# The second tail scores of a batch, issued ahead of the last slot block of the third pair of heads

## The chip, the cores and the metric

The kernel runs on one core of a Trainium2 chip. The metric is the device time of one execution in microseconds; the median of the runs counts. The engines are named as in the profile: PE (matrix multiplier) with PEld (its weight loads), DVE (vector engine), ACT (scalar engine, which does the exponentials), POOL (issues the row gathers and scatters), SP (issues the other transfers, in order). A line number such as L756 is a line of the kernel.

## The reference

Sixteen batches of 512 channels by 1024 tokens pass through one attention layer with 8 heads of 64, with keys and queries masked per token, and the layer's result is added to the input. Query, key and value are the same projection.

```python
xt = jnp.transpose(x, (0, 2, 1))
q = xt @ Wq.T
qh = q.reshape(B, T, NH, dk).transpose(0, 2, 1, 3)
scores = scale * jnp.einsum('bhqd,bhkd->bhqk', qh, qh)
logits = (scores * cmask + (1.0 - cmask) * NEG) * rmask
attn = jax.nn.softmax(logits, axis=-1)
ctx = jnp.einsum('bhqk,bhkd->bhqd', attn, qh)
out = ctx.transpose(0, 2, 1, 3).reshape(B, T, D) @ Wo.T
x = x + jnp.transpose(out, (0, 2, 1))
```

A masked query gets all logits zero, so its result is the mean of all values. A live query attends to the live keys alone. About half of the tokens are live.

## The kernel before, in words

**What is computed.** For each batch the kernel gathers the live tokens' rows into *slots* and works on these. A batch has `wide[b]` slots: 544 in batches 0 to 4, 528 in 5 to 13, 512 in 14 and 15. The first 512 are four *slot blocks* of 128; what is beyond, 32 or 16 slots, is the *tail*. Fourteen batches have one. The rows of masked tokens get the mean, added by `rest` (L874).

**Scores.** `scores(b, p, i)` (L653) with a block `i` of 0 to 3 takes one head `p`: four matmuls (L693) into a PSUM buffer `pss`, then one exponential on ACT (L697) into a tile `p`, with the row sums into `z`. There are two `pss` buffers, used in turn, and twelve `p` tiles. With `i` None it does a whole tail for four heads at once: 16 matmuls of 32 columns (L668), one exponential (L672), with row sums into `zt`; DVE then splits the result into a high part `hi` (L677) and a low part `lo` (L678), and four transfers (L684, L685) spread both over a tile `pt`, of which there is one. The first tail scores of a batch serve heads 0 to 3, the second heads 4 to 7.

**Attention and normalisation.** `attend(b, p, i, ps)` (L702) multiplies a block's probabilities with the values, for a pair `p` of heads (two of the eight heads; pairs 0 to 3): 8 matmuls L718 a block, 32 a pair. With `i` 4 it adds the tail from `pt` (L722) and copies the sum to a tile `c` (L726). Each pair needs reciprocals of its row sums: `recip_sums` (L734) computes them on DVE into `rcol` (L741 takes `z`, L747 takes `zt`, then L748, L749, L750); `recip_rows` (L752) transposes `rcol` on PE (L756), copies it out (L759, `rr`), writes it to DRAM (L761, `rd`) and reads it back spread over the partitions (L765, `rb`). `norm` (L769) multiplies `c` by `rb` (L791) and splits the result to 16 bits. `product` (L801) is the output projection: 12 matmuls L809 a slot block, whose result `plus` (L813, L814) adds to the gathered rows.

**The order.** `run` (L925) writes the order out by hand. A batch is a list `S` of 18 steps: the 16 blocks, pair by pair, and two tails put in between. In a step it runs first what the step before left for later (the transfers of `pt` and of the next queries' `xx`) and what the table `free` holds for this step's number; then the scores of the even head, a part of the list `m`, the scores of the odd head, one row transfer for POOL, another part of `m`. In a tail's step it is the tail scores and one part of `m`. The list `m` holds the rest of the work: of the batch before, the last normalisations and the projection; of the next batch, the row transposes (L481, with `xsplit`, L439 and L440), the query projections (L508), the values (L565), the row maxima (`top`, L620, and `bottom`, L629). How much of `m` goes into a part is set by costs that are written beside its entries and by the table `share` (L1100): 1.2 for a tail, 0.9 and 0.9 for the last block of a pair, 0.9 and 1.0 for the third, 1.0 and 0.6 for the first.

The attend matmuls of a pair run in the next pair's second block (L1131 to L1136), those on its tail in that pair's third block. `recip_sums` and `recip_rows` of the pairs 0 to 2 hang on the number `st` of the step of the pair's last block, `norm` of pair 2 runs in the next batch (from `second`, L1043), in batch 15 in the last step:

```python
                    if i == 3:
                        (whole if p < 3 else todo).append(L(self.attend, b, p, 4, None))
                        if p < 3:
                            free.setdefault(st + 2, []).append(L(self.recip_sums, b, p))
                            free.setdefault(st + 3, []).append(L(self.recip_rows, b, p))
```

**The planner.** The program is written in this order, and a framework then makes each engine's stream from it, before the run: at each point an engine takes, of what is ready by the framework's own estimate, what was written first. So DVE operations of neighbouring steps are found interleaved in the trace. On the chip an engine's stream is fixed.

Of the kernel before, what the change touches and what calls it, by code (L numbers as in the profile page):

```python
# [46 lines left out]
class Fast:  # L47
# [877 lines left out]
    def run(self, flag):  # L925
        B = self.B
        L = lambda f, *a: lambda: f(*a)
        S = [(p, i) for p in range(NP) for i in range(4)]
        S.insert(2, (0, None))
        S.insert(13, (1, None))  # L930
        N = len(S)

        def xt(n):
# [361 lines left out]
```

## Time and profile before

| | us |
|---|---|
| runs: median of three | 1044.05 |
| runs: lowest, highest | 1043.74, 5687.53 |
| profiled execution | 1045.58 |
| its span, first to last instruction | 1043.8 |

The granted clock of the profiled execution was 0.995. A batch takes about 62 us; the first tail scores of batch 5 start at 356.26 us and the second at 393.50, those of batch 6 at 419.73 and 458.56. The profile gives each engine's busy time, groups of instructions by line with their mean duration and the idle time ahead of them, and what ended that idle time. A wait for several things is put down to the one that came last by the profile, and it names the wrong one at times; the ends of matmuls are modelled, their starts are measured.

### The profile page before, as it was taken

To read this page: it belongs to the slowest core of one execution; us is meant where nothing else is said; L and a number is where in the kernel's file an instruction comes from. 1 tells how busy PE (TensorE), PEld (TensorE's weight loads), DVE (VectorE), ACT (ScalarE), POOL (GpSimd) and SP (SyncE) were. 2 spreads that over 40 slices of the span, in tenths; PEclk is the share of its full clock that TensorE was granted. 3 is DMA by queue.
4 is the path that set the end of the run, shared out by engine and by line. 5 is a ranking of instruction groups with operands and counts; after the bars stand their busy time and mean duration, and the time that the engine had idled before them with its cause. 6 is when DMAs were issued, how large, how long until landed. Compare 5 with 4: busy or idle time off the path is not lost. (4 is left out here: it accounts for less than half of the span.)

```text
span 1043.8 us, 23675 instructions
## 1 busy us (share of the span) xinstructions
PE 994.7 (95%) x8527; PEld 692.3 (66%) x8527; DVE 720.9 (69%) x2408; ACT 656.4 (63%) x1702; POOL 299.5 (29%) x308
## 2 busy tenths in 40 slices
PE   7798999999999999999999999999999999999995
PEld 6576667666666766667676666766767676776552
DVE  7897668666766657767666777667678675756562
ACT  5876666666666665757666557665766666655650
POOL 3101023223301222233222223223333322325652
PEclk9899999999999999999999999999999999999999
DMA  6756555557645576666558656565665566546641
GB/s 212 215 142 175 138 152 166 164 156 207 189 125 149 135 214 176 166 189 163 164 159 233 183 141 188 152 192 175 202 193 153 164 172 183 154 132 195 201 170 74
DMA packets 78796, 177.74 MB, mean 170 GB/s; under 512 B 14688, under 2 KB 20576, under 8 KB 78672
## 3 DMA queue, kind: packets, MB, share of 16 engines
q1 hardware_dynamic: 57584, 108.40, 38.3%
q0 software_dynamic: 21088, 67.75, 20.7%
q8 instruction: 70, 1.15, 0.5%
q14 instruction: 54, 0.44, 0.1%
HBM read 91.49 MB, written 33.91 MB: 120 GB/s over the span
## 5 line engine op out<-in xcount | busy, mean ns | idle before, releaser
L697 ACT ACTIVATE p<-pss,nm 128x528 f32<-128x528 f32 (+2 forms) x512 | 359.9, 707 | 190.6 <-PE pss L693 181.1
L693 PE MATMUL pss<-xx 128*128 128x264 f16 (+2 forms) x2048 | 302.7, 277 | 8.2 <-ACT p L697 7.0
L718 PE MATMUL pav<-p,v 128*64 128x264 f32 (+2 forms) x2048 | 243.3, 390 | 0.0
L693 PEld LDWEIGHTS <-xx 128*128 128x128 f16 x2048 | 195.0, 99 | 63.9 <-issue 26.8
L718 PEld LDWEIGHTS pav<-p,v 128*64 128x64 f32 x2048 | 141.4, 137 | 85.7 <-issue 13.3
L893 POOL DMA_INDIRECT y_out<-xa,idx x68 | 73.7, 1083 | 284.7 <-PE pss L693 129.4
L508 PE MATMUL pm<-xh,wqh 128*128 128x264 f16 (+5 forms) x512 | 142.4, 278 | 4.1 <-DVE xa L814 2.3
L508 PE MATMUL pm<-xl,wqh 128*128 128x264 f16 (+5 forms) x512 | 141.7, 277 | 0.2 <-DVE xl L440 0.2
L508 PE MATMUL pm<-xh,wql 128*128 128x264 f16 (+5 forms) x512 | 141.9, 277 | 0.0
L390 POOL DMA_INDIRECT xa<-x_in,idx x68 | 67.9, 998 | 203.1 <-PE pss L693 89.6
L508 PEld LDWEIGHTS <-wqh 128*128 128x128 f16 x1024 | 98.1, 99 | 24.5 <-issue 7.5
L697 ACT ACTIVATION_READ_ACCUMULATOR p<-pss,nm 128x1 f32 x512 | 104.1, 203 | 0.0
L893 POOL DMA_INDIRECT y_out<-xi,idx x60 | 71.5, 1192 | 101.4 <-PE pss L693 38.1
L809 PE MATMUL pm<-woh,ch 128*128 128x512 f16 x240 | 91.1, 379 | 0.0
L809 PE MATMUL pm<-woh,cl 128*128 128x512 f16 x240 | 90.9, 379 | 0.0
L809 PE MATMUL pm<-wol,ch 128*128 128x512 f16 x240 | 90.9, 379 | 0.0
L390 POOL DMA_INDIRECT xi<-x_in,idx x60 | 61.7, 1029 | 97.3 <-PE pss L693 33.8
L511 ACT ACTIVATE q<-pm 128x264 f32<-128x264 f32 (+5 forms) x128 | 50.3, 393 | 60.1 <-PE pm L508 59.8
L809 PEld LDWEIGHTS <-ch 128*128 128x128 f16 x480 | 45.9, 98 | 44.7 <-issue 0.9
L814 DVE SCALAR_TENSOR_TENSOR xa<-pm,xa 128x512 f32<-128x512 f32 x60 | 41.3, 688 | 44.3 <-PE pm L809 40.6
L880 DVE TENSOR_TENSOR xi<-xi,ub 128x512 f32<-128x512 f32 (+1 forms) x60 | 40.7, 687 | 44.2 <-PE pss L693 41.7
L791 DVE TENSOR_TENSOR c<-c,rb 128x528 f32<-128x528 f32 (+2 forms) x64 | 45.4, 710 | 32.8 <-PE pm L508 16.3
(220 smaller groups left out, 1511.4 us busy)
## 6 DMA issues: line engine op xcount, KB each, us to landing
xx<-hl SPq DMA_DIRECT2D x224, 136.0 KB
xm<-x_nat_in SPq DMA_DIRECT2D x56, 512.0 KB
rb<-rd SPq DMA_DIRECT2D x72, 132.0 KB
rb<-rd SPq DMA_DIRECT2D x40, 136.0 KB
pt<-c SPq DMA_DIRECT2D x36, 132.0 KB
pt<-p SPq DMA_DIRECT2D x36, 132.0 KB
ub<-ud SPq DMA_DIRECT2D x16, 256.0 KB
xx<-hl SPq DMA_DIRECT2D x32, 128.0 KB
```

What stands on the lines that cost most here:

```text
L390: dma = self.nc.gpsimd.indirect_dma_start(out=tile[:n], out_offset=None, in_=self.x, in_offset=bass.IndirectOffsetOnAxis(ap=idx, axis=0))
L508: self.beat = nc.tensor.matmul(pq, lhsT=w[:, c, e * P:(e + 1) * P], rhs=xx[:, c, cols], start=(k == 0), stop=(k == 3 * DC - 1)).ins
L511: nc.scalar.activation(s["q"][:, e, cols], pq, AF.Copy, scale=1.0 / (SX * SW))
L693: self.beat = nc.tensor.matmul(pt[:, g, :CH], lhsT=xx[:, 2 * k, i * P:(i + 1) * P], rhs=xx[:, 2 * k + a, g * CH:(g + 1) * CH], start=(a == ...
L697: self.exp = [nc.scalar.activation(t.rearrange("p (g c) -> p g c", g=2), pt[:, :, :CH], AF.Exp, bias=s["nm"][p // HG][:, p % HG:p % HG + 1 ...
L718: mm = nc.tensor.matmul(s["pav"][k * DK:(k + 1) * DK, g, :CH], lhsT=s["v"][p][:, i, k * DK:(k + 1) * DK], rhs=ps[k][:, cols], start=(i == ...
L791: self.once(nc.vector.tensor_tensor(c[:, :A], c[:, :A], s["rb"][p], ALU.mult), self.beat if p < 3 else None)
L809: nc.tensor.matmul(po[:cols.stop - cols.start], lhsT=a[:, e, cols], rhs=w[:, e, :], start=(e == 0 and k == 0), stop=(e == DC - 1 and k == 2))
L814: self.nc.vector.scalar_tensor_tensor(x, po, 1.0 / (SX * SW), x, ALU.mult, ALU.add)
L880: self.once(self.nc.vector.tensor_tensor(x[:n], x[:n], s["ub"][:n], ALU.add), self.beat)
L893: dma = self.nc.gpsimd.indirect_dma_start(out=self.out, out_offset=bass.IndirectOffsetOnAxis(ap=idx, axis=0), in_=x, in_offset=None)
```

## The change

The second tail is put into the list of steps one place earlier.

```diff
         S = [(p, i) for p in range(NP) for i in range(4)]
         S.insert(2, (0, None))
-        S.insert(13, (1, None))
+        S.insert(12, (1, None))
         N = len(S)
```

| step | before | after |
|---|---|---|
| 10, 11 | pair 2, blocks 1 and 2 | the same |
| 12 | pair 2, block 3 | second tail |
| 13 | second tail | pair 2, block 3 |
| 14 to 17 | pair 3, blocks 0 to 3 | the same |
| `recip_sums` of pair 2 | step 14 | step 15 |
| `recip_rows` of pair 2 | step 15 | step 16 |

The last two lines follow from `st + 2` and `st + 3`, as the block's own step is now 13. The entries of `free` that have a fixed number (loads of the batch after next at steps 0, 3, 6 and 9, their row sums on ACT at 4, 7, 10 and 13; in batch 0 the loads at 4, 7, 10 and 13) keep it: what is at step 13 now comes behind the tail and ahead of the block. In the two batches without a tail, the tail's step issues its part of `m` alone, and the `recip` steps of pair 2 move as in the others.

## The prediction

> **What bounds the kernel now.** I read the page first, then the windows by stage, the waits, and the timeline around the tail.
>
> ```profile
> PE 994.7 (95%) x8527; PEld 692.3 (66%) x8527; DVE 720.9 (69%) x2408; ACT 656.4 (63%) x1702; POOL 299.5 (29%) x308
> ...
> L697 ACT ACTIVATE p<-pss,nm 128x528 f32<-128x528 f32 (+2 forms) x512 | 359.9, 707 | 190.6 <-PE pss L693 181.1
> L693 PE MATMUL pss<-xx 128*128 128x264 f16 (+2 forms) x2048 | 302.7, 277 | 8.2 <-ACT p L697 7.0
> ```
>
> ACT waits 181.1 us for the scores; PE waits 7.0 us for ACT. The windows (length; then busy time with instruction count of PE, PEld, DVE, ACT, POOL; clock; DMA) say where PE is not full:
>
> ```profile
> 0.00:36.00 36.00, 28.02 (x298) 23.48 (x299) 26.70 (x100) 23.68 (x61) 12.47 (x33) 1.00 0.74 234
> 417.00:917.00 500.00, 487.33 (x4251) 342.58 (x4250) 352.76 (x1222) 322.65 (x838) 148.41 (x142) 1.00 0.62 174
> 979.00:1044.00 65.00, 51.10 (x342) 28.85 (x340) 27.61 (x71) 21.91 (x58) 30.00 (x28) 0.96 0.43 145
> ```
>
> In the eight batches of the middle line (about 62 us each) PE idles 12.67 us, 1.6 us a batch. Nothing but those gaps can be won by a new order, and nothing is lost unless PE gets new ones. Where are they near the tail? In batch 4 (start, duration, engine, line and what it does, idle before it):
>
> ```profile
> 333.81 0.30 DVE L747 TENSOR_TENSOR rcol<-zt,corr 32x1 f32<-32x1 f32 x2
> ...
> 334.87 0.28 PE L629 MATMUL pm<-ident,m 128*128 128x4 f32 x2
> ...
> 335.58 0.17 DVE L750 TENSOR_TENSOR rcol<-rcol,hit 128x10 f32<-128x10 f32 x1
> ...
> 335.89 0.30 PE L756 MATMUL pm<-ident,rcol 128*128 128x128 f32 x1 [0.74 <-ACT p L697]
> ```
>
> PE has passed L629 at 334.90 and stands until 335.89, with 0.10 us usual after an L629. The view names ACT, but L750, which writes what L756 reads, ends at 335.75, 0.14 us ahead. That is the wait. L756 is `recip_rows` of pair 2, and its sums take L747's operand `zt` from the exponentials of the second tail: tail scores 331.85, their exp 332.57 to 333.4, L747 333.81, L750, L756. The same 0.14 to 0.15 us stands between L750's end and L756 in batches 1, 3, 4, 6, 7, 9, 10, 12 and 13. One more wait on this tail, in batch 0, and one beside it:
>
> ```profile
> 87.75 0.49 PE L722 MATMUL pav<-pt,vt 128*128 128x272 f32 x2 [2.18 <-DMA pt<-p]
> ...
> 398.39 0.27 PE L508 MATMUL pm<-xh,wqh 128*128 128x264 f16 x1 [0.56 <-DVE xa L814]
> ```
>
> **The change, part by part.** Nothing is added or removed: 16 tail matmuls, one exp, two DVE operations and four `pt` transfers swap places with one slot block (8 matmuls, two exps). Fourteen batches have the tail. But the index of the block goes from 12 to 13, and `recip_sums` and `recip_rows` of pair 2 hang on that index: steps 14 and 15 become 15 and 16.
>
> *(A) The wait at L756.* The tail's exp comes a block (some 3 us) earlier, L756 one step later, behind the 32 attend matmuls of step 15 (336.59 to 340.08 in batch 4). With 3.5 to 4.4 us more between them and a need of 0.9, the wait goes. From the starts of L629 and L756: 0.96, 0.96, 0.99, 1.02, 1.01, 1.01, 1.01, 1.02 us in eight batches, less 0.10 each, 7.2 us; batch 13 adds 0.9: −8.1 us.
>
> *(B) Batch 0's `pt`.* The transfers were issued at 81.26 to 83.97 and PE stood 2.18 us for them. The tail moves up by the block that ran 71.98 to 74.93, some 3 us: −2.2. If the SP queue keeps them behind the `xx` transfers of 76.48 to 79.4, the gain is between 0 and −2.2; I take −2.0.
>
> *(C) L508 behind L814.* 2.3 us in all by the waits on L814, because DVE ran the tail's two operations (0.43 and 0.71) just before L814. They move ahead, but `project`, whose result L814 takes, may land between tail and block and meet them again: 0 to −2.3; I take −1.0, half.
>
> *(D) What is issued earlier or later with it.* The PSUM buffers of the scores alternate: the tail now waits for the exp of the block before, the moved block for the tail's, each an exp of 0.9 us on ACT. The trace has 15 waits of this kind among 512 half blocks, 7.0 us, 0.47 each. One fewer in a few batches would be −1, one more in each of 14 batches +6.6; I take four more, +2. On SP the four `pt` issues pass nothing but the `xx` transfers of the next query (396.22 to 398.62 in batch 5), whose reader runs some 10 us later. On POOL the row transfers keep one issue a step, and hang on the tail's last matmul in place of the block's: no PE work waits for them. ACT's row sum (L420, 1.24 us) changes from ahead of the tail's exp to ahead of the block's: cover is the 190.6 us in which ACT waits anyway.
>
> *(E) The later reciprocal.* L756 starts the chain copy, `rd` to DRAM, `rb` back, `norm` of pair 2 (L791) early in the next batch. In batch 5:
>
> ```profile
> 399.38 0.64 SPq L685 DMA_DIRECT2D pt<-p  x1
> 400.07 0.78 SPq L684 DMA_DIRECT2D pt<-c  x1
> 400.90 0.80 SPq L685 DMA_DIRECT2D pt<-p  x1
> 401.80 0.48 SPq L761 DMA_DIRECT2D rd<-rr  x1
> 407.03 1.10 SPq L765 DMA_DIRECT2D rb<-rd  x2
> ...
> 412.15 0.71 DVE L791 TENSOR_TENSOR c<-c,rb 128x528 f32<-128x528 f32 x1
> ```
>
> Here `rd` takes 5.23 us because it follows 528 KB of `pt`; for pair 1, with nothing ahead, 1.28 (388.42 to 389.70). Now L756 runs at 399.74 and L791 at 412.15, 12.4 us on. Moved behind the attends it would run at about 404.55, 7.6 us ahead of L791. The shortest chain in the trace, the last batch's, is 6.5 us (L756 1022.59, L791 1029.12, DVE idle 5.94 us for it). With the `pt` transfers already gone, 6.5 fits into 7.6: cost 0, and the cover left is 1.1 us. At the very end L791 of pair 2 (1014.34) would come about 3 us later, near 1017.5, its results near 1020.3, and PE takes them with the matmuls from 1021.28: 0 to +1 us, taken as 0.
>
> Sum: −8.1 −2.0 −1.0 +2 = −9.1 us.
>
> Should PE gaps count in full? The row: PE busy 97.5% in the middle window, and an L693 starts every 0.113 us without a pause. [...] The trace sides with the row, since the other engines wait for PE.
>
> The profiled execution took 1045.58 us (span 1043.8 and 1.8 around it), 1.5 over the median of 1044.05; the same sum taken off the median is 1044.05 − 9.1 = **1035 us**.
>
> **The rivals.**
> *1. The reciprocal comes too late (slower).* If `rd` still takes 5.23 us (behind `xx` or `xm` transfers), the chain is 6.5 + 4.0 = 10.5 against 7.6, and `norm` is 2.9 us late; if the whole shift of 4.8 us arrives, 4.8. Behind L791 on DVE stand L440 (413.52 to 414.80), which free the buffers for the transposes PE wants at 417.08: 2.3 us of cover. So from 2.3 us on it decides; at 4.8 PE loses 2.5 us in each of 13 batches, +32 us, less the 9: 1044 + 23 = 1067. For: 1.1 us of margin is small. Against: the `pt` bytes ahead of `rd` are what made it slow, and the planner places L791 by its own estimate of readiness. DVE ran nothing in the 5.94 us before the last L791. [...]
> *2. The gaps move (no change).* PE reaches the next buffer that DVE or ACT must free 0.9 us sooner and waits there. For: in batch 5's timeline DVE has no pause over 0.39 us from 390.75 to 402.4. Against: after L756 follow 3.5 us of attends, for which DVE need do nothing. A's 8.1 is paid again: 1035 + 8.1 = 1043; up to 1050 where D is at its end.
> *3. More is won.* All of A, B, C and none of D is −12.6, 1031; half of what is left of the 1.6 us a batch once A is out (8.1 over 14 is 0.6, so 1.0) is −7 more: 1024.
>
> **How the numbers follow.** Forecast (1031 to 1041) 0.52; gaps move (1041 to 1050) 0.28; late reciprocal (1050 to 1071) 0.13; more won 0.07. The range of 8 in 10 is 1029 to 1054: forecast, second rival and the nearer part of the first, 0.84. About 2%, 21 us, is what a measurement of this kernel can tell from no change: below 1023 only beyond rival 3, 0.04; above 1065 the far half of rival 1, 0.09; else 0.87.
>
> **What would show it.** A: L756 of pair 2 behind 32 L718, with no idle before it in batches 1, 3, 4, 6, 7, 9, 10, 12, 13. B: L722 near 86 us without its 2.18. C: the L814 entry of L508 below 2.3. E: second `rb` issue to L791 still near 4 to 5 us, `rd` to `rb` near 1.3 to 2.7 for pair 2, no DVE idle over 0.5 us before L791. It is wrong if PE's middle-window busy time does not rise, or if idle before L440 or L481 appears early in each batch.

## The result, and the profile after

| | before | after |
|---|---|---|
| median, us (16 runs each) | 1043.07 | 1050.47 |
| lowest, us | 1040.44 | 1045.18 |
| span of the profiled execution, us | 1043.8 | 1049.1 |

The changed kernel takes 1.0063 times the time of the one before (95% interval 1.0047 to 1.008): 0.6% slower, where 0.9% faster was forecast. This ratio is not the quotient of the medians (1.0071): it is worked out from the fast runs alone, which leaves out one run of 5687.53 us of the kernel before. Its interval, 0.33% wide, tells 0.6% from no change, where the prediction had allowed for 2%. First the page of after (busy us, share of the span; then groups with busy time, mean ns of one, and idle time ahead with what ended it):

```profile
PE 1000.3 (95%) x8527; PEld 693.9 (66%) x8527; DVE 719.4 (69%) x2408; ACT 653.7 (62%) x1702; POOL 298.6 (28%) x308
...
L693 PE MATMUL pss<-xx 128*128 128x264 f16 (+2 forms) x2048 | 303.8, 277 | 12.0 <-ACT p L697 6.4
...
L508 PE MATMUL pm<-xh,wqh 128*128 128x264 f16 (+5 forms) x512 | 142.7, 279 | 6.6 <-DVE xa L814 5.9
...
L791 DVE TENSOR_TENSOR c<-c,rb 128x528 f32<-128x528 f32 (+2 forms) x64 | 45.3, 708 | 56.6 <-DMA rb<-rd 21.7
```

Of before, a group and a line of the view of waits (us in all, times, longest):

```profile
L508 PE MATMUL pm<-xh,wqh 128*128 128x264 f16 (+5 forms) x512 | 142.4, 278 | 4.1 <-DVE xa L814 2.3
DVE c L791 <- DMA rb<-rd: 8.9, 7, 2.6
```

and from the windows of after:

```profile
417.00:917.00 500.00, 488.08 (x4241) 341.41 (x4239) 352.61 (x1226) 320.94 (x838) 149.63 (x142) 1.00 0.61 174
```

In the middle window PE is busy 488.08 us of 500, against 487.33: nearly as many gaps as before. PE's wait for L814 has gone from 2.3 to 5.9 us, all the idle time ahead of L693 from 8.2 to 12.0. L791's waits for `rb` are 21.7 us, 8.9 before.

**The wait at L756 is gone.** PE in batch 4 (start, duration, engine, line and what it does):

```profile
341.01 0.28 PE L629 MATMUL pm<-ident,m 128*128 128x4 f32 x2
...
347.25 0.28 PE L508 MATMUL pm<-xh,wql 128*128 128x266 f16 x1
347.36 0.27 PE L756 MATMUL pm<-ident,rcol 128*128 128x128 f32 x1
347.47 0.63 PE L693 MATMUL pss<-xx 128*128 128x272 f16 x4
```

L756 runs 6.3 us behind the L629 it followed directly before, 0.11 us from its neighbours on both sides, with no idle in brackets. The chain behind it, in batch 5 (SP and DVE in the timeline of after):

```profile
402.13 0.74 SPq L685 DMA_DIRECT2D pt<-p  x1
...
410.87 0.32 SPq L761 DMA_DIRECT2D rd<-rr  x1
412.16 1.62 SPq L765 DMA_DIRECT2D rb<-rd  x2
...
417.72 0.71 DVE L791 TENSOR_TENSOR c<-c,rb 128x528 f32<-128x528 f32 x1
```

`rd` takes 1.29 us to its `rb`, as forecast, in place of 5.23: the `pt` transfers are long gone.

**Batch 0 loses 5.9 us in the profiled execution.** The first attend matmul (L718) of batch 0 starts at 50.1 us before and 49.2 after, that of batch 1 at 115.2 and 120.2: this stretch takes 65.1 and 71.0. It begins on SP. The timeline of before, then of after:

```profile
76.48 0.48 SPq L536 DMA_DIRECT2D xx<-hl  x1
...
78.80 0.59 SPq L539 DMA_DIRECT2D xx<-hl  x1
...
81.26 0.48 SPq L684 DMA_DIRECT2D pt<-c  x1
```

```profile
75.25 1.91 SPq L684 DMA_DIRECT2D pt<-c  x2
77.27 1.18 SPq L685 DMA_DIRECT2D pt<-p  x2
78.48 0.60 SPq L536 DMA_DIRECT2D xx<-hl  x1
...
80.43 0.94 SPq L539 DMA_DIRECT2D xx<-hl  x1
```

The four `pt` transfers now stand ahead of the `xx` of the next query block, (1, 1), which is issued 2.0 us later although PE is 0.9 us earlier. On PE, in the timeline of after:

```profile
84.15 0.19 PE L565 MATMUL pm<-two,xx 128*128 128x64 f16 x1 [2.04 <-DMA xx<-hl]
84.18 0.28 PE L508 MATMUL pm<-xh,wqh 128*128 128x274 f16 x1
84.29 0.28 PE L508 MATMUL pm<-xl,wqh 128*128 128x274 f16 x1
...
85.14 0.43 PE L508 MATMUL pm<-xl,wqh 128*128 128x274 f16 x1
85.37 0.43 PE L508 MATMUL pm<-xh,wql 128*128 128x274 f16 x1
```

PE stands 2.04 us for `xx`; before, L565 started at 82.72 without a wait. Then the L508 start 0.23 us apart in place of 0.11: the granted clock has dropped to 0.50 (windows at the end). A second wait of this kind, 2.20 us, follows at 97.08. The whole stretch in the windows of before, of after and of run 4 below, which has the order of after in batch 0:

```profile
50.10:115.20 65.10, 60.96 (x561) 44.56 (x560) 56.16 (x197) 46.61 (x122) 5.32 (x5) 1.00 0.58 157
49.20:120.20 71.00, 64.47 (x559) 46.32 (x558) 56.63 (x197) 46.94 (x123) 5.28 (x5) 0.95 0.53 138
53.00:121.20 68.20, 61.34 (x559) 44.45 (x558) 56.74 (x197) 46.53 (x123) 5.65 (x5) 1.00 0.54 143
```

From before to after PE's idle time (length less busy time) grows from 4.1 to 6.5 us, 2.4 of the 5.9. The other 3.5 are in its busy time, at a granted clock of 0.95. In run 4 PE waits at the same two places (1.81 and 2.25 us), the clock stays at 1.00, and the stretch is 3.1 us longer than before. So, as an estimate from these stretches, the waits cost some 3 us, and the lowered clock as much again in this execution.

**The other batches gain little.** From the first attends of batch 1 to those of batch 13 the trace of before has 754.4 us and that of after 756.3, although eight of A's nine waits lie in this stretch. New waits pay them back. One is L508 behind L814, 12 times in place of 5. Batch 6, timeline of after:

```profile
463.92 0.43 DVE L677 CAST c<-p 128x528 fp32r<-128x528 f32 x1
...
464.61 0.70 DVE L678 TENSOR_TENSOR p<-p,c 128x528 fp32r<-128x528 f32 x1
...
465.23 0.70 DVE L528 TENSOR_TENSOR hl<-q,hl 128x528 f16<-128x528 f32 x1
465.72 0.38 PE L809 MATMUL pm<-woh,cl 128*128 128x512 f16 x1
...
466.13 0.63 DVE L747 TENSOR_TENSOR rcol<-zt,corr 16x1 f32<-16x1 f32 x4
466.79 0.69 DVE L814 SCALAR_TENSOR_TENSOR xa<-pm,xa 128x512 f32<-128x512 f32 x1
...
467.53 0.27 PE L508 MATMUL pm<-xh,wqh 128*128 128x264 f16 x1 [0.42 <-DVE xa L814]
```

The last L809 of this projection starts at 465.72, and L814, which takes its result, at 466.79: DVE is still at the tail's L677 and L678 and what they pushed back. In batch 4 of before the last L809 starts at 331.54 and L814 at 331.96, after 0.31 us in which DVE waited. The other new wait, 0.85 to 0.87 us of L693 for L672, stands at the start of batches 3, 6, 9 and 12; in all the view of waits of after has

```profile
PE pss L693 <- ACT p L672: 4.4, 9, 0.9
```

PE and ACT in the timeline of after, batch 6:

```profile
426.62 0.75 ACT L672 ACTIVATE p<-pss,nm 128x528 f32<-128x528 f32 x1
...
427.51 0.27 PE L693 MATMUL pss<-xx 128*128 128x264 f16 x1 [0.87 <-ACT p L672]
428.32 0.42 PE L481 MATMUL pm<-ident,xt 16*128 16x16 f32 x4 [0.54 <-DMA xt<-x_in,idx]
```

Together 1.4 us. L481 waits for a gather that GpSimd issues 11.2 us later than before (all work of this batch is some 7 us later), in the POOL timelines of before and of after:

```profile
413.71 0.86 POOL L390 DMA_INDIRECT xt<-x_in,idx  x1 [0.83 <-DVE c L792]
```

```profile
404.64 0.97 POOL L893 DMA_INDIRECT y_out<-xa,idx  x1 [2.61 <-issue]
...
424.91 0.86 POOL L390 DMA_INDIRECT xt<-x_in,idx  x1 [4.69 <-DVE xl L440]
```

One row transfer is issued a step. At step 13 the third part of the projection posts a scatter; it came ahead of that step's issue as long as that step was the tail (in a tail's step the first part of `m` is all of it), and comes behind it now that step 13 is a block and its second part of `m` follows the issue. The queue is then one longer, and the gather slides into the next batch.

### The profile page after: what moved, and what is told of

Read it like the earlier page. It is cut to its first block, busy times and chain, and to the rows that moved or that the text cites. A ratio compares the mean times of both kernels' runs of the same rounds, so it can differ in the third digit from the quotient of the medians.

```text
span 1049.1 us, 23657 instructions
## 1 busy us (share of the span) xinstructions
PE 1000.3 (95%) x8527; PEld 693.9 (66%) x8527; DVE 719.4 (69%) x2408; ACT 653.7 (62%) x1702; POOL 298.6 (28%) x308
## 5 line engine op out<-in xcount | busy, mean ns | idle before, releaser
L697 ACT ACTIVATE p<-pss,nm 128x528 f32<-128x528 f32 (+2 forms) x512 | 359.9, 708 | 199.1 <-PE pss L693 192.8
L693 PE MATMUL pss<-xx 128*128 128x264 f16 (+2 forms) x2048 | 303.8, 277 | 12.0 <-ACT p L697 6.4
L718 PE MATMUL pav<-p,v 128*64 128x264 f32 (+2 forms) x2048 | 243.8, 391 | 0.0
L693 PEld LDWEIGHTS <-xx 128*128 128x128 f16 x2048 | 194.1, 99 | 69.5 <-issue 30.3
L718 PEld LDWEIGHTS pav<-p,v 128*64 128x64 f32 x2048 | 141.5, 137 | 86.3 <-issue 14.0
L508 PE MATMUL pm<-xh,wqh 128*128 128x264 f16 (+5 forms) x512 | 142.7, 279 | 6.6 <-DVE xa L814 5.9
L508 PE MATMUL pm<-xh,wql 128*128 128x264 f16 (+5 forms) x512 | 142.1, 278 | 0.0
L508 PE MATMUL pm<-xl,wqh 128*128 128x264 f16 (+5 forms) x512 | 141.9, 277 | 0.2 <-DVE xl L440 0.2
L390 POOL DMA_INDIRECT xa<-x_in,idx x68 | 70.5, 1036 | 194.0 <-PE pss L693 82.1
L508 PEld LDWEIGHTS <-wqh 128*128 128x128 f16 x1024 | 97.4, 99 | 28.9 <-issue 11.5
L697 ACT ACTIVATION_READ_ACCUMULATOR p<-pss,nm 128x1 f32 x512 | 104.8, 205 | 0.0
L893 POOL DMA_INDIRECT y_out<-xi,idx x60 | 68.1, 1135 | 92.7 <-PE pss L693 30.0
L511 ACT ACTIVATE q<-pm 128x264 f32<-128x264 f32 (+5 forms) x128 | 50.5, 395 | 69.8 <-PE pm L508 68.5
L809 PE MATMUL pm<-woh,ch 128*128 128x512 f16 x240 | 91.0, 379 | 0.0
L809 PE MATMUL pm<-woh,cl 128*128 128x512 f16 x240 | 90.9, 379 | 0.0
L809 PE MATMUL pm<-wol,ch 128*128 128x512 f16 x240 | 90.9, 379 | 0.0
L791 DVE TENSOR_TENSOR c<-c,rb 128x528 f32<-128x528 f32 (+2 forms) x64 | 45.3, 708 | 56.6 <-DMA rb<-rd 21.7
L809 PEld LDWEIGHTS <-ch 128*128 128x128 f16 x480 | 46.2, 98 | 44.0
L814 DVE SCALAR_TENSOR_TENSOR xa<-pm,xa 128x512 f32<-128x512 f32 x60 | 41.0, 684 | 44.0 <-PE pm L809 40.2
```

The costliest lines, as they stand in the source:

```text
L390: dma = self.nc.gpsimd.indirect_dma_start(out=tile[:n], out_offset=None, in_=self.x, in_offset=bass.IndirectOffsetOnAxis(ap=idx, axis=0))
L508: self.beat = nc.tensor.matmul(pq, lhsT=w[:, c, e * P:(e + 1) * P], rhs=xx[:, c, cols], start=(k == 0), stop=(k == 3 * DC - 1)).ins
L511: nc.scalar.activation(s["q"][:, e, cols], pq, AF.Copy, scale=1.0 / (SX * SW))
L693: self.beat = nc.tensor.matmul(pt[:, g, :CH], lhsT=xx[:, 2 * k, i * P:(i + 1) * P], rhs=xx[:, 2 * k + a, g * CH:(g + 1) * CH], start=(a == ...
L697: self.exp = [nc.scalar.activation(t.rearrange("p (g c) -> p g c", g=2), pt[:, :, :CH], AF.Exp, bias=s["nm"][p // HG][:, p % HG:p % HG + 1 ...
L718: mm = nc.tensor.matmul(s["pav"][k * DK:(k + 1) * DK, g, :CH], lhsT=s["v"][p][:, i, k * DK:(k + 1) * DK], rhs=ps[k][:, cols], start=(i == ...
```

## The experiments

Three theories were put on record: 1, the loss is made once, in batch 0, by the order on SP; 2, by the later reciprocals; 3, by VectorE coming late to L814 in most batches. From the fifth run on, GpSimd's issue (3a) and VectorE's load (3b) are told apart. The stretches are measured in each run's trace between first attend matmuls, as above. Waits are PE's, in us. The eleven runs were made on three chips: the kernel before took 1054.31 us on that of runs 1 to 4, 1043.77 on that of runs 5 to 8 and 1044.10 on that of runs 9 to 11; so each ratio is to the kernel before on the same chip. Two ratios side by side are each known to about 0.2%, and the stretches of one trace each go beside them. The slower chip does not show in these stretches: where runs 3 and 4 have the order of before, they took 65.2 and 754.6. But some executions have a granted clock of 0.50 for 3.4 us, which adds 1.7 us by the estimate at the end. In the column of batches 1 to 12 that falls once into runs 5, 8 and 9 and twice into run 11. In runs 6, 7, 10 and 11 the waits of L565 are near 970 us, not in batch 0.

| run | ratio, 95% interval | batch 0 | batches 1 to 12 | L508 for L814 | L693 for L672 | L565 for `xx` |
|---|---|---|---|---|---|---|
| before | 1 | 65.1 | 754.4 | 2.3 | not listed | 0.2 |
| after | 1.0063, 1.0047 to 1.008 | 71.0 | 756.3 | 5.9 | 4.4 | 4.5 |
| 1: tail alone | 1.0055, 1.0039 to 1.0071 | 67.0 | 760.4 | 5.9 | 4.2 | 3.0 |
| 2: reciprocals alone | 0.9932, 0.9906 to 0.9957 | 66.0 | 748.8 | 2.2 | not listed | 1.1 |
| 3: not in batch 0 | 1.0031, 1.0011 to 1.0051 | 65.2 | 757.6 | 5.9 | 3.9 | not listed |
| 4: only in batch 0 | 1.0026, 1.0007 to 1.0044 | 68.2 | 754.6 | 2.2 | 0.3 | 4.3 |
| 5: `xx` first | 1.0040, 1.0024 to 1.0057 | 67.8 | 758.0 | 5.9 | 4.1 | 3.3 |
| 6: issue behind the block | 0.9993, 0.9977 to 1.0009 | 65.1 | 752.9 | 5.8 | 0.6 | 0.2 |
| 7: L677 on ScalarE | 1.0003, 0.9985 to 1.002 | 64.8 | 754.7 | 3.1 | 4.0 | 0.8 |
| 8: 5, 6 and 7 together | 0.9974, 0.9959 to 0.9990 | 65.9 | 755.5 | 2.7 | 0.8 | 2.9 |
| 9: split behind `hl` | 1.0023, 1.0010 to 1.0037 | 64.9 | 758.2 | 5.9 | 4.2 | 2.0 |
| 10: 6 and 7 | 0.9980, 0.9963 to 0.9997 | 64.3 | 751.8 | 2.6 | 0.6 | 0.8 |
| 11: L677 on ScalarE, before | 1.0028, 1.0009 to 1.0047 | 65.2 | 757.9 | 0.3 | not listed | 0.2 |

**Run 1, the tail alone.** The changed kernel with the reciprocals of pair 2 back at steps 14 and 15:

```diff
-                            free.setdefault(st + 2, []).append(L(self.recip_sums, b, p))
-                            free.setdefault(st + 3, []).append(L(self.recip_rows, b, p))
+                            free.setdefault(st + 2 - (p == 2), []).append(L(self.recip_sums, b, p))
+                            free.setdefault(st + 3 - (p == 2), []).append(L(self.recip_rows, b, p))
```

> The tail one place earlier in all batches, the reciprocals of pair 2 at their old steps 14 and 15. Theory 1 (the loss is made once, in batch 0, where four pt transfers now stand on SP ahead of the xx transfers that PE waits for): the two waits of L565 near 84 and 97 us stay, the first attend matmul of batch 0, pair 3 comes near 100 us instead of 95.9, and the time is 1046 to 1052. Theory 2 (the later reciprocals make DVE wait in L791 for rb, and that costs PE): with the old steps the loss is gone, 1036 to 1044. Theory 3 (with the tail in its new place DVE is late with L814 and PE waits at L508 in most batches): L508's idle for L814 stays near 5.9 us against 2.3 before, and the time is above 1046 also where batch 0 is as before.

It is 0.55% slower than before. L791 waits only 6.6 us for `rb`, and the loss is there all the same, against theory 2. The waits of L508 and L693 are those of the changed kernel (5.9 and 4.2 us), so they belong to the tail's place. Batch 0 loses 1.9 us in place of 5.9. The order on SP is that of the changed kernel (`pt` from 80.57, `xx` from 83.61), and L565 waits 2.39 us at 89.81; but the second wait is 0.28 us in place of 2.20, and the granted clock stays at 1.00.

**Run 2, the reciprocals alone.** The kernel before, with those of pair 2 one step later:

```diff
+                            free.setdefault(st + 2 + (p == 2), []).append(L(self.recip_sums, b, p))
+                            free.setdefault(st + 3 + (p == 2), []).append(L(self.recip_rows, b, p))
```

> The tail in its old place, only the reciprocals of pair 2 one step later (15 and 16). Theory 1: no loss in batch 0, and the wait of PE at L756 in nine batches is gone: 1035 to 1040. Theory 2: slower than before, 1046 to 1052, with 20 us or more of DVE idle before L791 for rb. Theory 3: L508's idle for L814 as before, 2.3 us; time 1035 to 1040 as well.

Run 2 (six executions) is 0.7% faster than before, and faster than the changed kernel: the best of this study. Groups of run 2, as above:

```profile
L508 PE MATMUL pm<-xh,wqh 128*128 128x264 f16 (+5 forms) x512 | 142.3, 278 | 2.8 <-DVE xa L814 2.2 <-DVE nm L631 0.4
...
L791 DVE TENSOR_TENSOR c<-c,rb 128x528 f32<-128x528 f32 (+2 forms) x64 | 45.4, 710 | 46.7 <-DMA rb<-rd 23.3 <-PE pm L508 13.4 <-SPq L1265 4.8
```

DVE waits 23.3 us for `rb` here, more than in the changed kernel, and the kernel is faster: theory 2 falls. In both runs the view of waits no longer lists L756 behind ACT (6.0 before). Either half of the change takes that wait away, so the gain is had once, and run 2 puts it at some 0.7%. What is left to the tail's place is a loss: 1.0063 to 0.9932, about 1.3% by two ratios from two chips, with the reciprocals late in both.

**Runs 3 and 4, where the loss is.** Run 3 is the kernel before until batch 0 is through, and the changed one from then on; run 4 the other way round. Run 3's edit, to the kernel before, ahead of each batch's steps (run 4: the changed kernel, with the numbers 13 and 12 exchanged):

```diff
+                if b == 1:
+                    S.insert(12, S.pop(13))
```

> The change in all batches but batch 0, which keeps the old order. Theory 1: the 5.8 us that batch 0 lost are back, 1043 to 1046, and the runs lie as close together as before. Theories 2 and 3 (a loss in every batch): 1047 to 1052.

> The change in batch 0 alone. Theory 1: nearly all of the loss, 1047 to 1051, with waits for xx at L565 near 84 and 97 us and windows of half clock behind them. Theories 2 and 3: 1042 to 1044.

Both are slower than before, 0.3% each, and add to about the whole. Batch 0 is one half, in run 4's first stretch (68.2 against 65.1); the other half is in run 3's second (757.6 against 754.4), with L508's 5.9 us. Neither theory 1 nor 3 suffices alone.

**Run 5, `xx` ahead of `pt`.** The changed kernel, with

```diff
-                    for f in soon + free.get(st, []):
+                    for f in (soon[::-1] if st == 13 else soon) + free.get(st, []):
```

> The changed kernel, but at step 13 the two transfers that were left for later are issued in the other order, those of `xx` of the next query block ahead of the four of `pt`, as in the kernel before. Theory 1a (the loss of batch 0 is the `pt` transfers that wait on SP for VectorE's `lo`, with `xx` behind them): in batch 0 L565 of the query block (1, 1) no longer waits for `xx` (2.0 and 2.2 us of PE's waits go), the time from the first attends of batch 0 to those of batch 1 falls from 71.0 to about 67 us, and the ratio to the kernel before falls from 1.0063 to about 1.003 (1.002 to 1.004). Rival (the order on SP is not it: the tail's other work makes batch 0 late): L565's wait goes or is met at another line, batch 0 still takes 70 us or more and the ratio stays at 1.005 to 1.007.

The ratio is at the upper end of theory 1a's range, but the mechanism was hit in part: L565 still waits 3.2 us in batch 0, and that takes 67.8, nearer to the 67 of theory 1a than to the 70 of its rival. A granted clock of 0.50 from 96.3 on is, by the estimate at the end, 1.7 of these us. In this run's trace one `pt` transfer (76.48) still goes ahead of the first `xx` (77.07), and `hl`, which `xx` copies, is finished at 77.92 against 76.62 before: L677 and L678 run between L527 and L529. Run 9 takes both away.

**Run 6, GpSimd's issue behind the block.** Run 3's kernel, with, at step 13, the second part of `m` ahead of the issue:

```diff
+                    late = (i, st) == (3, 13)
+                    if late:
+                        fill(share[st][1])
                     for _ in range(1 if b < B - 2 else -(-len(self.urgent + self.spare) // (N - st))):
                         self.issue()
...
-                    fill(share[st][1])
+                    if not late:
+                        fill(share[st][1])
```

> The third run's kernel (batch 0 in the order of before, all other batches changed), but at step 13 GpSimd's next issue is made behind the slot block, where project(.,2) has already posted its scatter, so that this scatter goes out no step later than before. Theory 3a (in batches 2, 5, 8 and 11 GpSimd's queue is one issue longer, the gather of a row slides into the next batch, and the start of batches 3, 6, 9 and 12 waits some 1.3 us each, 4 to 5 us in all): the waits of L693 for L672 (4.4 us) and of L481 for `xt` go, and the ratio falls from 1.0031 to 0.998 to 1.000. Rival (those waits only move to another line, since PE is behind the same work): the waits go or change their line, and the ratio stays at 1.002 to 1.005.

POOL's timeline of run 6:

```profile
413.80 0.86 POOL L390 DMA_INDIRECT xt<-x_in,idx  x1 [0.83 <-DVE c L792]
```

The gather is back in its batch, L693's wait for L672 is 0.6 us, the 12 batches take 4.7 us less than in run 3, and the ratio falls by 0.38% to 0.9993. Theory 3a holds, and its rival falls: the wait did not move to another line.

**Run 7, L677 on ScalarE.** Run 3's kernel, with

```diff
-            nc.vector.tensor_copy(hi, t)
+            (nc.scalar.copy if p == 1 and b else nc.vector.tensor_copy)(hi, t)
```

> The third run's kernel, but the second tail's rounding to `hi` (L677) is made by ScalarE in place of VectorE from batch 1 on. Theory 3b (VectorE, with the tail's L677 and L678 now ahead of the block, comes late to L814, and PE's L508 waits for that): the waits of L508 for L814 fall from 5.9 to 2 to 4 us and the ratio from 1.0031 to 0.999 to 1.001. Rival (L814 is late because of the L809 behind which it stands, or ScalarE becomes late in its place): L508's waits stay above 5 us, or waits for ScalarE take their place, and the ratio stays at 1.002 to 1.005.

L508 waits 3.1 us for L814 in place of 5.9, the stretch is 2.9 us shorter, the ratio 1.0003. Theory 3b holds for that part.

**Run 8, the edits of runs 5, 6 and 7 together**, in the changed kernel.

> The changed kernel with the three edits of this call together (`xx` ahead of `pt` on SP, GpSimd's issue of step 13 behind the slot block, L677 of the second tail on ScalarE from batch 1 on). If the three causes are all of the loss, what is left is the gain of the later reciprocals, which alone measured 0.9932, and the wait of L756 that goes: ratio 0.993 to 0.998, with L565's, L693's and L508's added waits all gone. If the tail ahead of the block costs by itself in the steady batches whatever stands on the queues: 1.000 to 1.004.

The ratio is in the range of the first case, at its upper end; of the added waits, L693's and L508's are gone, but L565's 2.9 us in batch 0 is not, as in run 5. In the profiled execution batch 9 took 68.5 us (66.2 before), which is why its second stretch is long: L693 waits 1.37 and 1.11 us for L697 at 628.33 and 630.05, and from 630.0 to 633.4 the granted clock is 0.50.

**Run 9, batch 0 settled.** The changed kernel, with, in batch 0, the rounding behind the `hl` copies and all `pt` behind the `xx`:

```diff
+            late = (b, p) == (0, 1)
+            def split():
+                with self.behind(self.last_hl) if late else ExitStack():
+                    nc.vector.tensor_copy(hi, t)
+                    nc.vector.tensor_tensor(lo, t, hi.bitcast(F32), ALU.subtract)
+            if not late:
+                split()
             def spread():
+                if late:
+                    split()
...
+                with self.behind(self.last_xx) if late else ExitStack():
...
-                    for f in soon + free.get(st, []):
+                    for f in (soon[::-1] if (b, st) == (0, 13) else soon) + free.get(st, []):
```

> The changed kernel, but in batch 0 the rounding of the second tail (L677, L678) and its four `pt` transfers stand behind the `hl` copies (L527 to L529) and all four `xx` transfers of the next query block; the tail's matmuls and its exponential stay ahead of the block. The fifth run had moved only three of the four `pt` transfers, and `hl` still came 1.3 us later for the L677 and L678 between its copies. Theory 1b (the loss of batch 0 is these two engines' orders, VectorE's and SP's, and nothing else): the time from the first attends of batch 0 to those of batch 1 falls from 71.0 to 65 to 66.5 us (before 65.1), L565's waits for `xx` of block (1, 1) go, a wait of L722 for `pt` of some 2 us may come back, and the ratio falls from 1.0063 to 1.002 to 1.004, that of the third run. Rival (the tail's matmuls or its exponential ahead of the block make it late as well): 67.5 us or more as in the fifth run (67.7), ratio 1.004 or more.

SP's timeline of run 9:

```profile
74.68 0.48 SPq L536 DMA_DIRECT2D xx<-hl  x1
...
76.70 0.60 SPq L539 DMA_DIRECT2D xx<-hl  x1
77.39 0.56 SPq L694 DMA_DIRECT2D pt<-c  x1
```

Batch 0 takes 64.9 us and the ratio is 1.0023. The tail's matmuls and exponential stand where the change put them, so these cost batch 0 nothing that shows; its loss comes from the order on two engines, with the lowered clock (0.95 over the stretch in after) behind the waits. The forecast of L565's waits was met in part: of the 2.0 us left, 1.6 are at the next query block (91.10). L722 did not wait for `pt`.

**Run 10, the two edits of the other batches together**, runs 6 and 7 on run 3's kernel.

> The third run's kernel (batch 0 in the order of before, the others changed) with both edits of the steady batches, GpSimd's issue of step 13 behind the block and L677 of the second tail on ScalarE. Theory 3 (the two causes add): from 1.0031 by 0.38 and 0.28 per cent to 0.995 to 0.998, and the stretch from the first attends of batch 1 to those of batch 13 from 757.6 to 750 to 752 us. Rival (ScalarE, with the rounding too, is late in its turn, so the second edit is worth little beside the first): 0.998 to 1.001, the stretch at 752.5 us or more, L693's waits for L697 above 5 us in these batches.

Waits of PE in run 10 from 417 to 917 us (in all, times, longest):

```profile
PE pss L693 <- ACT p L697: 2.6, 5, 0.7
PE pm L508 <- DVE xa L814: 1.0, 2, 0.5
```

The ratio, 0.9980, is the end of the one range and the beginning of the other; the stretch, 751.8, is in theory 3's, and L693 does not wait more for ScalarE (3.6 us from 120 to 917, where the rival had over 5). Together they take 0.51% off, where 0.66 was their sum; each of these is known to about 0.3%, so that says neither that they add in full nor that they do not.

**Run 11, a control.** Run 7's edit in the kernel before.

> The kernel before, with L677 of the second tail on ScalarE from batch 1 on, and nothing else: a control for the seventh run. Theory 3b (that edit gained because the tail's earlier place had made VectorE late): with the tail in its old place there is nothing to gain, L508's waits for L814 stay at 2.3 us and the ratio is 0.998 to 1.002. Rival (relieving VectorE of the rounding is a gain wherever the tail stands): 0.996 or less.

A miss for both: 1.0028. The wait of L508 for L814 went, from 2.3 to 0.3, but another came, in the view of waits of run 11:

```profile
PE pav L722 <- DMA pt<-p: 11.7, 10, 2.4
```

With the tail in its old place ScalarE finishes `hi` up to 0.7 us later behind the tail's exponential (1.29 us in place of 0.62 in batch 7), and PE gets to L722 some 8 to 9 us behind that exponential; in run 7 it gets there some 12 us behind it and, from batch 1 on, does not wait. Why 0.7 us makes waits of up to 2.44 is not shown. Two of the waits (2.44 us at 529.14, 1.87 at 719.36) are followed by a granted clock of 0.50 for 3.4 us, and the batches with them, 7 and 10, take 67.4 and 67.1 us for 64.3 and 64.1: more than all of the 3.5 us by which the stretch is longer than before. So the edit's gain in run 7 needs the earlier tail, which leaves time for it; in the kernel before, relieving VectorE is paid for at L722.

## Why the prediction was wrong

**What held.** (A) happened as described. Its size is seen alone in run 2: 0.68%, 7.1 us of 1043 (4.5 to 9.8 by the interval), against 8.1. (B) happened: L722 runs at 88.09 without a wait. (E) was right in its cost and in the time: L756 of pair 2 to L791 is 7.50 us in batch 5, where 7.6 was worked out, and 6.6 to 8.6 in batches 1 to 15. It was wrong that DVE would not stand: in eight batches L791 of pair 2 waits 0.65 to 2.55 us for `rb`; but PE has cover for that, as run 2 shows. The first rival, which made the late reciprocal dear, falls with it.

**What failed, by its steps.**

*(D) SP.* "On SP the four `pt` issues pass nothing but the `xx` transfers of the next query … whose reader runs some 10 us later." That was read off batch 5. In batch 0 the reader, L565, starts 3.3 us after the last `xx` is issued (79.39 to 82.72 before). Batch 0 pays 5.9 us in the profiled execution; with orders mended (run 9) the ratio falls from 1.0063 to 1.0023. (B) had named this very order, but only as a bound on its own gain. And the sum counted each wait of PE at its own length ("nothing is lost unless PE gets new ones"): here 3.5 of the 5.9 us are no gap, but matmuls at a lowered clock (0.95 over the stretch) behind two gaps.

*(C).* −1.0 us was taken, between 0 and −2.3; L508's waits for L814 grew by 3.6. The text had the mechanism ("may land between tail and block and meet them again") and left the loss out of its bound. Run 7 takes 2.8 us of these waits away and gains 2.9.

*(D) POOL.* "No PE work waits for them" was true for a transfer a step later, and false for a queue one longer: the last gather of the batch falls into the next. Run 6 puts this at 4.7 us.

*(D) buffers.* +2 was taken for L693 behind L697; it went from 7.0 to 6.4, nothing. Behind L672, the tail's own exponential, five short waits came, 0.9 us in all.

**The second rival**, "the gaps move", is the case that came: 1050 is the upper end of its 1041 to 1050. But what paid A back was not PE reaching a busy buffer 0.9 us sooner. It was the order on three engines, SP, VectorE and GpSimd, that the tail was moved past. The measured 1050 lies in the wide range, 1029 to 1054, by this rival's number and not by its mechanism. As an estimate, from sizes of different runs, the parts add up: −7.1 for (A) by run 2, +5.9 for batch 0, in which (B)'s gain is contained, +3.6 for L508 and +4.7 for GpSimd by run 6 are +7.1 us, where 0.63% of 1043 is 6.6.

**What stays open.** With both edits of runs 6 and 7, and batch 0 as before, the kernel is at 0.9980; with the tail in its old place and the reciprocals late, at 0.9932. The two ratios come from two chips, and their difference of 0.5% is known to about 0.3%. In the traces 751.8 and 748.8 us stand against each other in the 12 batches, with PE's idle time 12.5 and 12.0; 1.3 of the 3.0 us are batch 10 of run 10 (65.2, where runs 6, 7 and 8 have 63.8 or 63.9). So the tail's earlier place may cost something more than these runs explain; no single wait shows it.

## What to carry to other kernels

A step that moves takes its transfers, its vector work and its position relative to a once-a-step issue along with it: check each queue it passes at the tightest batch, here the first, not at a typical one. Where an edit does two things, cost each alone; here the side effect, later reciprocals, would have had the gain by itself, and the edit proper took the same wait away and lost more than that elsewhere.

## What the runs showed of the hardware

In after, two waits of PE for `xx`, of 2.04 and 2.20 us, have a lowered clock behind them. Windows of after behind these two, then one of before behind its wait for `pt` (length; busy time of PE, PEld, DVE, ACT, POOL; granted clock, DMA share, GB/s):

```profile
84.80:88.20 3.40, 3.40 (x24) 2.43 (x21) 1.21 (x3) 1.47 (x3) 0.00 (x0) 0.50 0.40 127
98.50:101.90 3.40, 3.40 (x16) 2.32 (x18) 3.02 (x8) 2.88 (x8) 0.00 (x0) 0.50 0.36 82
86.00:90.00 4.00, 2.25 (x19) 1.97 (x20) 3.25 (x11) 1.48 (x5) 1.17 (x2) 1.00 0.66 176
```

The granted clock is 0.50 for 3.4 us in each of the first two; half of that, 1.7 us, is what one such stretch takes from a PE that is always busy (an estimate from the window). Twelve L508 take 1.87 us from first start to last in place of 1.28, with the first six still at the old distance. The same 3.4 us of 0.50 stand in run 8 behind two waits close together, 1.37 and 1.11 us, in run 9 behind 0.87 and 1.02 (421.3 to 424.7), and in run 11 behind 2.44 and, later, behind 1.87 us. The kernel before has an idle of 2.18 us ahead of 87.75 and keeps a clock of 1.00 from 86 to 90, and so do runs 1 and 3 in batch 0 with 2.39 and 2.32 us; so the length of the idle alone does not decide: 1.87, 2.04, 2.20 and 2.44 us have a clock of 0.50 behind them; 2.18, 2.32 and 2.39 us, and the 1.81 and 2.25 of run 4, have not. What else decides is not shown.
